# Attention over a node graph in fp32: the two heads of a pair computed side by side on TensorE

## The chip, the cores and the metric

The kernel runs on one core of a Trainium2 chip. The metric is the device time of one launch in microseconds (us), as the median of the runs. A profile of one execution on the same core comes with it. In it, PE is TensorE's matmul stream, PEld its loading of the stationary operand, DVE is VectorE, ACT is ScalarE, POOL is GpSimd and SP is SyncE.

## The reference

There are two layers over x[16, 1024, 256] (batch, nodes, channels), all in fp32, with one weighted adjacency matrix adj[1024, 1024] for all batches.

```python
# layer 0, HEADS = 4, hd = 64
fea = transpose(x, (0, 2, 1));  c_adj = mean(fea, axis=1)
diff = c_adj[:, None, :] - c_adj[:, :, None]
A = abs(abs(sigmoid(diff) - 0.5) - 0.5) * 2.0          # made symmetric
g = relu(einsum('bcn,bnm->bcm', fea, adj * A) * para)
q = heads of transpose(g);  k, v = heads of x @ kv_w
attn = softmax(einsum('bhnd,bhmd->bhnm', q, k) * scale, axis=-1)
out = einsum('bhnm,bhmd->bhnd', attn, v)
x = layernorm(x + out)
# layer 1: h = relu(x w_loop + adj (x w_neigh) + b), twice (256 -> 128 -> 256)
x = layernorm(x + (x + h) * 0.5)
```

The change lies in the attention of layer 0: for each batch and head, a 1024 by 1024 table of scores over 64 channels, its softmax over the last axis, and the product with the 64-wide values.

## The kernel before, in words

All constants, both forms of adj among them, stay on chip, and the kernel goes through the 16 batches in a Python loop that is written out into one straight program. A batch's 1024 nodes lie as eight blocks of 128 partitions. The steps of a batch are `attention`, a LayerNorm, `project` of the next batch (keys, values, and queries from the graph product `g_ps`), `graph_conv`, a second LayerNorm, and the store.

A tile framework assigns buffers from named pools. A pool tag has a fixed number of buffers (`bufs`), and an instruction that writes a new tile waits until the last reader of the tile that had the buffer is done. The framework also chooses the order in which the instructions stand on each engine; an engine then executes its own list in that order. So the order of the source isn't the order on PE: scores of a later tile stand between transposes and value products of an earlier one.

In `attention` the four heads are two pairs. The channels of a pair fill the 128 partitions: head s=0 has rows 0 to 63, head s=1 rows 64 to 127. A group is one pair and one half `j` of the nodes (512 queries, four blocks `i`). In a group, one head after the other does this:

- Scores (line 216): for each block `i`, two matmuls of 512 columns write a tile of 128 by 1024 into PSUM (`big`, two buffers of two banks each). The contraction is over 64 rows, so a matmul uses the upper or the lower half of the array's rows.
- Softmax: VectorE takes the negated maximum (line 219), ScalarE the exponential with the row's sum (line 221), into a `probs` tile (six buffers). The tile in PSUM is then free.
- For each of eight blocks `mt` of the keys: four transposes (line 226) into one bank (`bank`, three buffers), a copy to `pT` (lines 72 and 74, VectorE and ScalarE in turn; three buffers), and a value product (line 229) of 512 columns that accumulates into `pav[rows]`. It has 64 output channels, so it uses the left or the right half of the array's columns. `pav` has one buffer (tag `av`).

After both heads, `pav` is copied to `oT` (line 232), transposed back (line 237), scaled by the reciprocal of the sums and added to x (line 242). `wg` in `project` (lines 190 to 192) has three buffers of the size of a `probs` tile.

Of the kernel before, what the change touches and what calls it, by code (L numbers as in the profile page):

```python
# [10 lines left out]
F32 = mybir.dt.float32  # L11
AF = mybir.ActivationFunctionType
ALU = mybir.AluOpType
AX = mybir.AxisListType
# [3 lines left out]
def kernel(  # L18
# [11 lines left out]
    b2: bass.AP,  # L30
    out: bass.AP,
):
    """Graph attention with a LayerNorm, then a two-step graph convolution with a LayerNorm.

    A batch's nodes n = t * 128 + p lie on partition p, block t. The channel-major
    forms (suffix T) hold channels on partitions and nodes along the free axis.
    Everything of a batch stays on chip from its load to its store.
    """
    nc = tc.nc

    B, N, C = x.shape
# [18 lines left out]
    def big_psum(name):  # L60
        return psum.tile([P, N], F32, tag="big", name=name, bufs=2)
# [4 lines left out]
    turn = [0]  # L66

    def evacuate(dst, src):
        """Copy from PSUM, on the scalar and the vector engine in turn."""
        turn[0] ^= 1  # L70
        if turn[0]:
            nc.vector.tensor_copy(dst, src)  # L72
        else:
            nc.scalar.copy(dst, src)  # L74
# [3 lines left out]
        nc.sync.dma_start(out=xb, in_=x[b].rearrange("(t p) c -> p t c", p=P))  # L78
        return xb

# [1 line left out]
    x_next = load_x(0)  # L82
    adj_sb = const.tile([P, NT, N], F32, name="adj_sb")
    adj_v = adj.rearrange("(t p) m -> p t m", p=P)
# [38 lines left out]
                evacuate(adjT_sb[:, mt, ts(j, FB)], pt)  # L123

    def to_channel_major(src, name):
        """[node, channel] blocks to [channel, node]."""
        dst = work.tile([P, NC, N], F32, tag="xT", name=name, bufs=2)
        for cc in range(NC):
            for j in range(NJ):
                pt = bank_psum(f"{name}_ps_{cc}_{j}")  # L130
                for i in range(TJ):
                    nc.tensor.transpose(pt[:, ts(i, P)], src[:, j * TJ + i, ts(cc, P)], ident)  # L132
                evacuate(dst[:, cc, ts(j, FB)], pt)
        return dst

    def layernorm(xb, name):
        """In place over the channels of every node."""
        mv = small.tile([P, NT, 2], F32, tag="mv", name=f"mv_{name}", bufs=2)
        for t in range(NT):
            st = small.tile([P, nc.vector.BN_STATS_DIM], F32, tag="st", name=f"st_{name}_{t}")  # L140
            nc.vector.bn_stats(st, xb[:, t, :])
            nc.vector.bn_aggr(mv[:, t, :], st)
        rstd = small.tile([P, NT], F32, tag="rstd", name=f"rstd_{name}", bufs=2)
        nc.vector.tensor_scalar_add(rstd, mv[:, :, 1], EPS)
        nc.gpsimd.tensor_tensor(rstd, rstd, neg_half, ALU.pow)
        for t in range(NT):
            nc.vector.tensor_scalar(xb[:, t, :], xb[:, t, :], mv[:, t, 0:1], rstd[:, t:t + 1],  # L147
                                    op0=ALU.subtract, op1=ALU.mult)

    def project(b, xb):  # L150
        """Queries from the channel-weighted graph, keys and values of a batch."""
        xT = to_channel_major(xb, f"xT_{b}")

        # The channel mean of each node: along the free axis on all partitions, and per partition.
        pc = big_psum(f"mean_ps_{b}")
        for j in range(NJ):
            for cc in range(NC):
                nc.tensor.matmul(pc[:, ts(j, FB)], mean_w, xT[:, cc, ts(j, FB)],
                                 start=(cc == 0), stop=(cc == NC - 1))
        c_row = work.tile([P, N], F32, tag="c_row", name=f"c_row_{b}")  # L160
        nc.scalar.copy(c_row, pc)
        c_sum = small.tile([P, NT], F32, tag="c_sum", name=f"c_sum_{b}", bufs=2)
        nc.vector.tensor_reduce(c_sum, xb, AX.X, ALU.add)
        neg_c = small.tile([P, NT], F32, tag="neg_c", name=f"neg_c_{b}", bufs=2)
        nc.vector.tensor_scalar_mul(neg_c, c_sum, -1.0 / C)

        kT = work.tile([P, NC, N], F32, tag="kT", name=f"kT_{b}")
        for kb in range(NC):
            pk = big_psum(f"k_ps_{b}_{kb}")
            for j in range(NJ):  # L170
                for cc in range(NC):
                    nc.tensor.matmul(pk[:, ts(j, FB)], kvw_sb[:, cc, ts(kb, P)], xT[:, cc, ts(j, FB)],  # L172
                                     start=(cc == 0), stop=(cc == NC - 1))
            nc.scalar.copy(kT[:, kb, :], pk)

        v = work.tile([P, NT, C], F32, tag="v", name=f"v_{b}")
        per = N // C
        for g in range(NT // per):
            pv = big_psum(f"v_ps_{b}_{g}")
            for i in range(per):  # L180
                for cc in range(NC):
                    nc.tensor.matmul(pv[:, ts(i, C)], xT[:, cc, ts(g * per + i, P)], kvw_sb[:, cc, C:2 * C],  # L182
                                     start=(cc == 0), stop=(cc == NC - 1))
            nc.scalar.copy(v[:, g * per:(g + 1) * per, :], pv.rearrange("p (i c) -> p i c", c=C))

        # A[n, m] = 2 (0.5 - |sigmoid(d) - 0.5|) = 1 - tanh(|d| / 2), d = c[m] - c[n]; it is symmetric.
        pg = [big_psum(f"g_ps_{b}_{cb}") for cb in range(NC)]
        for t in range(NT):
            wg = work.tile([P, N], F32, tag="wg", name=f"wg_{b}_{t}", bufs=3)
            nc.scalar.activation(wg, c_row, AF.Abs, bias=neg_c[:, t:t + 1])  # L190
            nc.scalar.activation(wg, wg, AF.Tanh, scale=-0.5)  # L191
            nc.vector.scalar_tensor_tensor(wg, wg, 1.0, adj_sb[:, t, :], op0=ALU.add, op1=ALU.mult)  # L192
            for cb in range(NC):
                for j in range(NJ):
                    nc.tensor.matmul(pg[cb][:, ts(j, FB)], xb[:, t, ts(cb, P)], wg[:, ts(j, FB)],  # L195
                                     start=(t == 0), stop=(t == NT - 1))
        qT = work.tile([P, NC, N], F32, tag="qT", name=f"qT_{b}")
        for cb in range(NC):
            nc.vector.tensor_mul(qT[:, cb, :], pg[cb], para_sb[:, cb, :])
            nc.scalar.activation(qT[:, cb, :], qT[:, cb, :], AF.Relu, scale=QSCALE)  # L200
        return qT, kT, v

    def attention(b, xb, qT, kT, v):
        """Adds the heads' outputs to xb."""
        for pair in range(NC):
            for j in range(NJ):
                pav = psum.tile([P, FB], F32, tag="av", name=f"av_{b}_{pair}_{j}", bufs=1)
                den = small.tile([P, TJ, 2], F32, tag="den", name=f"den_{b}_{pair}_{j}", bufs=2)
                for s in range(2):
                    rows = slice(s * HD, (s + 1) * HD)  # L210
                    probs = []
                    for i in range(TJ):
                        t = j * TJ + i
                        ps = big_psum(f"s_{b}_{pair}_{t}_{s}")
                        for mj in range(NJ):
                            nc.tensor.matmul(ps[:, ts(mj, FB)], qT[rows, pair, ts(t, P)],  # L216
                                             kT[rows, pair, ts(mj, FB)], start=True, stop=True)
                        nmax = small.tile([P, 1], F32, tag="nmax", name=f"nmax_{b}_{pair}_{t}_{s}")
                        nc.vector.tensor_reduce(nmax, ps, AX.X, ALU.max, negate=True)  # L219
                        pr = work.tile([P, N], F32, tag="probs", name=f"pr_{b}_{pair}_{t}_{s}", bufs=6)  # L220
                        nc.scalar.activation(pr, ps, AF.Exp, bias=nmax, accum_out=den[:, i, s:s + 1])  # L221
                        probs.append(pr)
                    for mt in range(NT):
                        pt = bank_psum(f"pT_ps_{b}_{pair}_{j}_{s}_{mt}")
                        for i in range(TJ):
                            nc.tensor.transpose(pt[:, ts(i, P)], probs[i][:, ts(mt, P)], ident)  # L226
                        pT = work.tile([P, FB], F32, tag="pT", name=f"pT_{b}_{pair}_{j}_{s}_{mt}", bufs=3)
                        evacuate(pT, pt)
                        nc.tensor.matmul(pav[rows, :], v[:, mt, pair * P + s * HD:pair * P + (s + 1) * HD], pT,  # L229
                                         start=(mt == 0), stop=(mt == NT - 1))  # L230
                oT = work.tile([P, FB], F32, tag="oT", name=f"oT_{b}_{pair}_{j}", bufs=2)
                nc.scalar.copy(oT, pav)
# [11 lines left out]
                            xb[:, t, cols], op0=ALU.mult, op1=ALU.add)  # L244

    def graph_conv(b, xb):
        """Two graph convolutions on xb, and xb + (xb + h) / 2 into it."""
        xT = to_channel_major(xb, f"x1T_{b}")

        p1 = big_psum(f"t1_ps_{b}")  # L250
# [15 lines left out]
        h1T = work.tile([HID, N], F32, tag="h1T", name=f"h1T_{b}")  # L266
        nc.scalar.activation(h1T, ph, AF.Relu, bias=b1_sb)

        # adj (h1 w2) is taken as (adj h1) w2: h1 is half as wide.
        h1 = work.tile([P, NT, HID], F32, tag="hid", name=f"h1_{b}")  # L270
        for j in range(NJ):
            pt = bank_psum(f"h1n_ps_{b}_{j}")
# [67 lines left out]
```

## Time and profile before

| what | value |
|---|---|
| median of 2 runs | 4411.66 us (4403.0 and 4420.31) |
| span of the profiled execution | 4400.6 us |
| mean granted clock of TensorE | 0.987 |
| PE busy | 4244.0 us (96%) |
| PEld busy | 1872.7 us (43%) |
| DVE busy | 1618.8 us (37%) |
| ACT busy | 1448.9 us (33%) |

The profiled execution's span runs from its first to its last instruction. A launch's time has something around that span: the two runs lie 2.4 and 19.7 us above it. In the groups of the profile, a line names the source line, the engine, the operation, what is written and read with the shape, and the number of records; after the bar come the busy time and the mean length of one record, and then the idle time of that engine just ahead of the group, with what ended most of it. Matmuls are pipelined, so a record's length is more than the distance from its start to the next one's start.

### The profile page before, as it was taken

The page shows a single profiled execution, that of the slowest core. Times are in us where ns is not written, and L with a number is a line of the kernel's source. Part 1 is how long each engine was busy: PE and PEld are TensorE (multiplying, and loading weights), DVE is VectorE, ACT ScalarE, POOL GpSimd, SP SyncE. Part 2 cuts the span into 40 slices and gives each one's busy share as a digit, 9 for nine tenths or more (in the row PEclk, how much of TensorE's full clock was granted, in tenths as well). Part 3 has the DMA queues.
Part 4 walks back from the last instruction along what each step waited for, and adds up shares of the span by engine and source line. Part 5 has one row for each costly group of instructions (what it writes and reads, how often), then busy time and mean ns, then how long its engine had stood idle before and what let it go on. Part 6 is the DMA issues. An engine that isn't in the chain of part 4 may idle for free. (4 is left out here: it accounts for less than half of the span.)

```text
span 4400.6 us, 33372 instructions
## 1 busy us (share of the span) xinstructions
PE 4244.0 (96%) x13504; PEld 1872.7 (43%) x13504; DVE 1618.8 (37%) x2752; ACT 1448.9 (33%) x2161; POOL 53.4 (1%) x41
## 2 busy tenths in 40 slices
PE   8999999999999999999999999999999999999997
PEld 4344443444434344343443434434344343443433
DVE  3424434243342433424333243343433424344242
ACT  3333323334233342333423234233332333333231
POOL 0000000000000000000000000000000000000000
PEclk9999999999999999999999999999999999999999
DMA  2000000000000000000000000000000000000000
GB/s 77 1 1 19 1 20 0 0 20 1 20 1 0 20 1 19 1 1 19 1 19 1 1 20 1 20 1 10 10 1 19 1 12 8 1 19 1 10 0 10
DMA packets 36044, 41.98 MB, mean 10 GB/s; under 512 B 817, under 2 KB 34354, under 8 KB 35890
## 3 DMA queue, kind: packets, MB, share of 16 engines
q1 hardware_dynamic: 34802, 36.18, 2.5%
q10 hardware_dynamic: 1088, 3.67, 0.2%
q8 instruction: 106, 1.74, 0.2%
q14 instruction: 48, 0.39, 0.0%
HBM read 23.07 MB, written 16.78 MB: 9 GB/s over the span
## 5 line engine op out<-in xcount | busy, mean ns | idle before, releaser
L216 PE MATMUL s<-kT,qT 64*128 64x512 f32 x2048 | 1068.5, 630 | 8.7 <-ACT pr L221 8.7
L229 PE MATMUL av<-pT,v 128*64 128x512 f32 x2048 | 1034.8, 620 | 13.6 <-DVE pT L72 6.1
L219 DVE TENSOR_REDUCE nmax<-s 128x1 f32<-128x1024 f32 x512 | 625.9, 1222 | 667.8 <-PE s L216 665.8
L221 ACT ACTIVATE pr<-s,nmax 128x1024 f32<-128x1024 f32 x512 | 571.6, 1116 | 698.3 <-DVE nmax L219 698.2
L226 PEld LDWEIGHTS pT_ps<-ident,pr 128*128 128x128 f32 x4096 | 438.1, 141 | 684.0 <-issue 527.8
L226 PE MATMUL pT_ps<-ident,pr 128*128 128x128 f32 x4096 | 640.1, 285 | 44.1 <-ACT pr L221 36.9
L74 ACT COPY pT<-pT_ps 128x512 f32<-128x512 f32 x512 | 293.8, 587 | 1030.2 <-PE pT_ps L226 843.8
L72 DVE COPY pT<-pT_ps 128x512 f32<-128x512 f32 x512 | 346.9, 688 | 729.9 <-PE pT_ps L226 572.9
L216 PEld LDWEIGHTS s<-kT,qT 64*128 64x128 f32 x2048 | 332.8, 187 | 396.5 <-issue 348.6
L229 PEld LDWEIGHTS av<-pT,v 128*64 128x64 f32 x2048 | 233.8, 138 | 556.8 <-issue 233.6
L195 PE MATMUL g_ps<-wg,x 128*128 128x512 f32 x1024 | 442.1, 592 | 0.0
L195 PEld LDWEIGHTS g_ps<-wg,x 128*128 128x128 f32 x1024 | 194.6, 190 | 238.1 <-issue 233.4
L192 DVE SCALAR_TENSOR_TENSOR wg<-wg,adj_sb 128x1024 f32<-128x1024 f32 x128 | 156.0, 1225 | 358.0 <-ACT wg L191 358.0
L264 PE MATMUL h_ps<-adjT_sb,t 128*128 128x512 f32 x512 | 226.5, 595 | 3.6 <-ACT t L256 3.6
L279 PE MATMUL u_ps<-adjT_sb,h 128*128 128x512 f32 x512 | 224.0, 595 | 6.0 <-DVE h L72 3.7
L190 ACT ACTIVATE wg<-c_row,neg_c 128x1024 f32<-128x1024 f32 x128 | 145.1, 1145 | 115.8 <-PE g_ps L195 115.3
L242 DVE SCALAR_TENSOR_TENSOR x<-o_ps,rden,x 128x64 f32<-128x64 f32 x512 | 104.0, 276 | 150.1 <-PE o_ps L237 150.1
L264 PEld LDWEIGHTS h_ps<-adjT_sb,t 128*128 128x128 f32 x512 | 96.0, 190 | 131.3 <-issue 115.0
L279 PEld LDWEIGHTS u_ps<-adjT_sb,h 128*128 128x128 f32 x512 | 96.0, 190 | 124.6 <-issue 114.8
L72 DVE COPY h<-h1n_ps 128x512 f32<-128x512 f32 x16 | 11.1, 692 | 368.7 <-PE h1n_ps L274 368.7
L191 ACT ACTIVATE wg<-wg 128x1024 f32<-128x1024 f32 x128 | 134.2, 1054 | 2.5
L172 PE MATMUL k_ps<-xT,kvw_sb 128*128 128x512 f32 x256 | 113.8, 592 | 0.0
(68 smaller groups left out, 2043.5 us busy)
## 6 DMA issues: line engine op xcount, KB each, us to landing
x<-in_x_dram SPq DMA_DIRECT2D x16, 1024.0 KB, 5.7
out_dram<-x SPq DMA_DIRECT2D x16, 1024.0 KB, 4.4
adj_sb<-in_adj_dram SPq DMA_DIRECT2D x2, 1024.0 KB, 17.4
adj_sb<-in_adj_dram ACTq DMA_DIRECT2D x2, 1024.0 KB, 9.2
para_sb<-in_L_gnn_para_dram ACTq DMA_DIRECT2D x1, 1024.0 KB, 17.9
kvw_sb<-in_L_gnn_kv_w_dram ACTq DMA_DIRECT2D x1, 512.0 KB, 6.0
w1l_sb<-in_L_gnn_w_loop_dram SPq DMA_DIRECT2D x1, 128.0 KB, 19.1
w1n_sb<-in_L_gnn_w_neigh_dram SPq DMA_DIRECT2D x1, 128.0 KB, 15.1
```

The costliest lines, as they stand in the source:

```text
L72: nc.vector.tensor_copy(dst, src)
L74: nc.scalar.copy(dst, src)
L190: nc.scalar.activation(wg, c_row, AF.Abs, bias=neg_c[:, t:t + 1])
L192: nc.vector.scalar_tensor_tensor(wg, wg, 1.0, adj_sb[:, t, :], op0=ALU.add, op1=ALU.mult)
L195: nc.tensor.matmul(pg[cb][:, ts(j, FB)], xb[:, t, ts(cb, P)], wg[:, ts(j, FB)], start=(t == 0), stop=(t == NT - 1))
L216: nc.tensor.matmul(ps[:, ts(mj, FB)], qT[rows, pair, ts(t, P)], kT[rows, pair, ts(mj, FB)], start=True, stop=True)
L219: nc.vector.tensor_reduce(nmax, ps, AX.X, ALU.max, negate=True)
L221: nc.scalar.activation(pr, ps, AF.Exp, bias=nmax, accum_out=den[:, i, s:s + 1])
L226: nc.tensor.transpose(pt[:, ts(i, P)], probs[i][:, ts(mt, P)], ident)
L229: nc.tensor.matmul(pav[rows, :], v[:, mt, pair * P + s * HD:pair * P + (s + 1) * HD], pT, start=(mt == 0), stop=(mt == NT - 1))
L264: nc.tensor.matmul(ph[:, ts(j, FB)], t1[:, mt, :], adjT_sb[:, mt, ts(j, FB)], start=False, stop=(mt == NT - 1))
L279: nc.tensor.matmul(pu[:, ts(j, FB)], h1[:, mt, :], adjT_sb[:, mt, ts(j, FB)], start=(mt == 0), stop=(mt == NT - 1))
```

## The change

The two heads of a pair go through a group together. For each block `i`, the score matmuls alternate between head 0 and head 1 in the source (upper rows, lower rows), into two `big` tiles that are allocated together. All eight `probs` tiles of a group are made before the first value product in the source. For each `mt`, both heads' transposes and copies come first and then both value products, one into the left and one into the right columns' half of `pav`. `probs` and `wg` now share one tag `row` with ten buffers in place of six and three; `pT` has four buffers in place of three. The numbers and shapes of matmuls, transposes, copies, maxima and exponentials are the same as before.

```diff
-            wg = work.tile([P, N], F32, tag="wg", name=f"wg_{b}_{t}", bufs=3)
+            wg = work.tile([P, N], F32, tag="row", name=f"wg_{b}_{t}", bufs=10)
...
-                for s in range(2):
-                    rows = slice(s * HD, (s + 1) * HD)
-                    probs = []
-                    for i in range(TJ):
-                        t = j * TJ + i
-                        ps = big_psum(f"s_{b}_{pair}_{t}_{s}")
-                        for mj in range(NJ):
-                            nc.tensor.matmul(ps[:, ts(mj, FB)], qT[rows, pair, ts(t, P)],
+                heads = [slice(s * HD, (s + 1) * HD) for s in range(2)]
+                probs = {}
+                for i in range(TJ):
+                    t = j * TJ + i
+                    ps = [big_psum(f"s_{b}_{pair}_{t}_{s}") for s in range(2)]
+                    for mj in range(NJ):
+                        for s, rows in enumerate(heads):
+                            nc.tensor.matmul(ps[s][:, ts(mj, FB)], qT[rows, pair, ts(t, P)],
                                              kT[rows, pair, ts(mj, FB)], start=True, stop=True)
+                    for s in range(2):
                         nmax = small.tile([P, 1], F32, tag="nmax", name=f"nmax_{b}_{pair}_{t}_{s}")
-                        nc.vector.tensor_reduce(nmax, ps, AX.X, ALU.max, negate=True)
-                        pr = work.tile([P, N], F32, tag="probs", name=f"pr_{b}_{pair}_{t}_{s}", bufs=6)
-                        nc.scalar.activation(pr, ps, AF.Exp, bias=nmax, accum_out=den[:, i, s:s + 1])
-                        probs.append(pr)
-                    for mt in range(NT):
+                        nc.vector.tensor_reduce(nmax, ps[s], AX.X, ALU.max, negate=True)
+                        pr = work.tile([P, N], F32, tag="row", name=f"pr_{b}_{pair}_{t}_{s}", bufs=10)
+                        nc.scalar.activation(pr, ps[s], AF.Exp, bias=nmax, accum_out=den[:, i, s:s + 1])
+                        probs[s, i] = pr
+                for mt in range(NT):
+                    pTs = []
+                    for s in range(2):
                         pt = bank_psum(f"pT_ps_{b}_{pair}_{j}_{s}_{mt}")
                         for i in range(TJ):
-                            nc.tensor.transpose(pt[:, ts(i, P)], probs[i][:, ts(mt, P)], ident)
-                        pT = work.tile([P, FB], F32, tag="pT", name=f"pT_{b}_{pair}_{j}_{s}_{mt}", bufs=3)
+                            nc.tensor.transpose(pt[:, ts(i, P)], probs[s, i][:, ts(mt, P)], ident)
+                        pT = work.tile([P, FB], F32, tag="pT", name=f"pT_{b}_{pair}_{j}_{s}_{mt}", bufs=4)
                         evacuate(pT, pt)
-                        nc.tensor.matmul(pav[rows, :], v[:, mt, pair * P + s * HD:pair * P + (s + 1) * HD], pT,
+                        pTs.append(pT)
+                    for s, rows in enumerate(heads):
+                        nc.tensor.matmul(pav[rows, :], v[:, mt, pair * P + s * HD:pair * P + (s + 1) * HD], pTs[s],
                                          start=(mt == 0), stop=(mt == NT - 1))
```

## The prediction, made before the result was known

> **What bounds the kernel now.** I read the page first, its engine shares and then its costliest groups:
>
> ```profile
> PE 4244.0 (96%) x13504; PEld 1872.7 (43%) x13504; DVE 1618.8 (37%) x2752; ACT 1448.9 (33%) x2161; POOL 53.4 (1%) x41
> ...
> L216 PE MATMUL s<-kT,qT 64*128 64x512 f32 x2048 | 1068.5, 630 | 8.7 <-ACT pr L221 8.7
> L229 PE MATMUL av<-pT,v 128*64 128x512 f32 x2048 | 1034.8, 620 | 13.6 <-DVE pT L72 6.1
> L219 DVE TENSOR_REDUCE nmax<-s 128x1 f32<-128x1024 f32 x512 | 625.9, 1222 | 667.8 <-PE s L216 665.8
> L221 ACT ACTIVATE pr<-s,nmax 128x1024 f32<-128x1024 f32 x512 | 571.6, 1116 | 698.3 <-DVE nmax L219 698.2
> ...
> L226 PE MATMUL pT_ps<-ident,pr 128*128 128x128 f32 x4096 | 640.1, 285 | 44.1 <-ACT pr L221 36.9
> ```
>
> TensorE is the bound; VectorE and ScalarE wait for it. Scores (S, L216) use half the rows of the array (64*128), value products (V, L229) half its columns (128*64). Each has 1024 matmuls in the source and 2048 records here: an fp32 matmul is two records. Together they hold 2103 of 4244 busy us, and PE waited only 66.4 us (8.7+13.6+44.1) ahead of S, V and the transposes of the probabilities (T).
>
> Next, the timeline of PE inside a batch (start, length, records):
>
> ```profile
> 410.67 1.53 PE L226 MATMUL pT_ps<-ident,pr 128*128 128x128 f32 x12
> 412.16 2.79 PE L229 MATMUL av<-pT,v 128*64 128x512 f32 x6
> 414.88 1.09 PE L226 MATMUL pT_ps<-ident,pr 128*128 128x128 f32 x8
> 415.90 1.12 PE L216 MATMUL s<-kT,qT 64*128 64x512 f32 x2
> 416.96 1.93 PE L229 MATMUL av<-pT,v 128*64 128x512 f32 x4
> 418.82 3.70 PE L216 MATMUL s<-kT,qT 64*128 64x512 f32 x8
> 422.45 1.45 PE L226 MATMUL pT_ps<-ident,pr 128*128 128x128 f32 x9
> ```
>
> From start to next start, six V records take 2.72 us and four 1.86: 0.43 for each record, and 0.15 for each run whatever its length. S gives the same 0.43 and 0.2 a run (3.63 for eight, 1.06 for two); T gives 0.11 and 0.15 (1.49 for twelve, 1.02 for eight). A half-array record is thus as slow as a full one, and every change between S, V and T costs 0.15 to 0.2 us.
>
> Third, the timeline of what a score tile waits for, and the windows by stage:
>
> ```profile
> 420.83 1.22 DVE L219 TENSOR_REDUCE nmax<-s 128x1 f32<-128x1024 f32 x1 [2.55 <-PE s L216]
> ...
> 422.09 1.11 ACT L221 ACTIVATE pr<-s,nmax 128x1024 f32<-128x1024 f32 x1 [2.56 <-DVE nmax L219]
> ...
> 423.11 0.19 ACT L221 ACTIVATION_READ_ACCUMULATOR pr<-s,nmax 128x1 f32 x1
> ```
>
> ```profile
> 400.44:441.19 40.75, 40.65 (x133) 15.92 (x134) 16.88 (x25) 14.38 (x26) 0.00 (x0) 1.00 0.00 0
> ...
> 363.00:370.00 7.00, 7.00 (x10) 1.78 (x10) 0.56 (x1) 1.91 (x4) 0.00 (x0) 0.54 0.62 197
> ```
>
> A score tile is free for the next one 2.5 us after its last record (1.22, 0.03, 1.11, 0.1 for the accumulator's end, 0.05 to PE). The first window is one group (a pair, a half j of the nodes): 40.75 us, PE busy 40.65. The second shows the clock at 0.54 after a wait:
>
> ```profile
> 362.36 0.68 PE L226 MATMUL pT_ps<-ident,pr 128*128 128x128 f32 x3 [1.17 <-ACT pr L221]
> ```
>
> [...]
>
> **The change part by part.**
>
> *Alternation.* [...] I counted the neighbours in the orders of the two built programs. Before has none. After has 497 V alternations, but only 151 S ones, since the scheduler mostly gives each score tile both its 512-column halves at once, often with transposes before the other head.
>
> Of the 497, 377 have two or more transposes, or a score run, between the transposes of the second operand and the first product. Its copy (0.69 on VectorE, 0.59 on ScalarE) is then done about when B could start: I take 0.35 us, 377 x 0.35 = 132. The other 120 have that copy still running for 0.75 to 0.85 us after A starts, against 0.91 for A alone: 0.12 each, 14. Sum −146 us. I give S nothing: its alternations lie where the next score tile waits for its buffer (below); the other bound is 151 x 0.32 = 48.
>
> *Fewer runs.* S runs fall from 664 to 473, V runs from 616 to 527, transpose runs after them from 856 to 826: 191 x 0.2 + 89 x 0.15 + 30 x 0.15 = −56 us.
>
> *A longer score phase.* Before, four score tiles belong to a half-group, two computed ahead, and the other head's products fill the waits. Now eight stand together, and only three transposes of each i fit between (three banks). I laid one group out by hand from the durations above, t=0 at the last score run before the final products. First score 0 to 1.05; products to 2.91; oT's copy (3.05 to 3.64) precedes that tile's exponential on ScalarE, so its buffer frees at 4.9. Scores 2.91 to 3.96, o transposes to 4.55, scores of both heads to 7.31. On VectorE the eight L242 operations (1.63) stand ahead of the next maximum: 4.66 to 6.28, maximum to 7.5, exponential to 8.8. PE has three transposes to 7.79, then waits 1.02. Scores 8.81 to 12.43, transposes to 12.9, wait 0.47 for the buffer at 13.37; scores of i=3, then 0.25 for the last head-0 exponential; the last head-1 one is hidden by the next group's first scores. Sum 1.74 us, against 1.0 on average (66.4/64): +0.74 x 64 = +47. Bounds: 0 (all covered) to 3 us a group, +130.
>
> *Buffers.* probs and wg share ten tiles of 1024 where they had six and three: eight are live and two ahead, as before four and two. g_ps's matmuls had no idle time ahead (0.0); wg is done long before probabilities want its tiles. 0. pT with four instead of three: 0. No DMA is moved, and SP and POOL keep their order.
>
> *Clock.* The mean is 0.987: 1.3% of 4400 is 57 us, mostly one low stretch near each batch's start (1.17 us wait). There the new order has a score tile every 1.8 us and shorter waits, which may save 30; [...] I take 0, and keep −30 to +170.
>
> Sum: −146 −56 +47 = −155 on the profiled 4400.6, so 4246 as a span. The runs are 2.4 to 19.7 us above that span, their median 11.1: 4411.7 − 155 = 4257, −3.5%. 2% (88 us) is about what a measurement tells from no change.
>
> **The rivals.**
>
> *No overlap in fp32.* The 146 go: 4403, no change. For it: nothing in this trace shows two tiles at once. [...]
>
> *Every alternation restarts like a run: slower.* [...] 497 x 0.15 + 151 x 0.2 = 105 us come on top of 4403: 4508. Place: between the two products of each mt. From 0.15 us an alternation it decides (648 x 0.15 = 97, to 4500). For: the first record of each run in this trace exposes its load. [...]
>
> *The throttle.* The 1.02 us wait lies among scores[...]. If each of 64 groups loses 3.4 us less the 0.7 of waits it then covers, 173: 4430 with overlap, 4576 without. [...]
>
> **How the numbers follow.** Overlap 0.54 (4257; own range 4205 to 4325); no overlap 0.23 (4403); restart 0.13 (4508); throttle 0.10 (4430 or 4576, half each). Faster by 2% is below 4323: nearly all of the first, 0.51. Slower is above 4500: restart and half of the throttle, 0.19. Within: 0.30. The range 4200 to 4500 leaves out some 0.06 below and 0.14 above.
>
> **What would show it.** In the timeline, a V run of four should take 1.5 us to the next start where before's took 1.86, with the second head's first record starting about 0.1 us after the first head's second. The busy time of the V group should fall by some 150 us and that of S by little; idle time ahead of S should rise from 8.7 to about 100 us, released by the exponential. An unchanged 0.43 between all V records means no overlap; over 0.5 at the change of head means restarts. A mean clock below 0.97 means the throttle. I am wrong most easily on fp32 tiles not overlapping, or on VectorE's order making the score phase wait longer.

## The result, and the profile after

The changed kernel takes 4557.1 us (median of two runs, 4554.8 to 4559.3) against 4411.7 before: 1.034 times as long, with a 95% interval of 1.031 to 1.037. The profiled execution spans 4557.6 us. The forecast was 4257, with a range to 4500.

The page of the kernel after, its engine shares, the granted clock in 40 slices, and the three PE groups of attention (line 218 scores, 236 value products, 231 transposes):

```profile
PE 4302.4 (94%) x13504; PEld 1944.0 (43%) x13504; DVE 1612.1 (35%) x2752; ACT 1433.1 (31%) x2161; POOL 53.4 (1%) x41
...
PEclk8897987989879898798988989789897898978888
...
L218 PE MATMUL s<-kT,qT 64*128 64x512 f32 x2048 | 1211.1, 792 | 135.1 <-ACT pr L224 134.6
L236 PE MATMUL av<-pT,v 128*64 128x512 f32 x2048 | 865.5, 668 | 28.7 <-DVE pT L72 9.3
...
L231 PE MATMUL pT_ps<-ident,pr 128*128 128x128 f32 x4096 | 690.7, 306 | 1.7 <-DVE x L249 0.4
```

The value products did fall, from 1034.8 busy us to 865.5. The scores rose from 1068.5 to 1211.1, and the wait ahead of them from 8.7 to 135.1. The new thing is the clock: its mean is 0.888 where it was 0.987. In the clock records of both traces every stretch is at half clock or at full, so that is 2 x 0.112 x 4558 = 1021 us at half clock, against 2 x 0.013 x 4401 = 114 before.

The timeline of PE in one group shows both sides, first the overlap, then the loss:

```profile
399.31 1.56 PE L236 MATMUL av<-pT,v 128*64 128x512 f32 x4
400.81 0.87 PE L231 MATMUL pT_ps<-ident,pr 128*128 128x128 f32 x6
...
402.66 1.08 PE L236 MATMUL av<-pT,v 128*64 128x512 f32 x4
403.67 1.12 PE L218 MATMUL s<-kT,qT 64*128 64x512 f32 x2
...
407.47 0.55 PE L231 MATMUL pT_ps<-ident,pr 128*128 128x128 f32 x3
409.47 4.87 PE L218 MATMUL s<-kT,qT 64*128 64x512 f32 x8 [1.45 <-ACT pr L224]
414.27 0.90 PE L231 MATMUL pT_ps<-ident,pr 128*128 128x128 f32 x3
415.10 3.78 PE L218 MATMUL s<-kT,qT 64*128 64x512 f32 x4
```

Four product records took 1.86 us to the next start before. Here they take 1.50 where the second head's copy comes late (399.31), and 1.01 where both operands are ready (402.66): two slots for four records, a full overlap. Ready pairs are the minority: of the 394 such runs at full clock in the trace, 72 took 1.01 us, 72 took 1.37, 146 took 1.49 and 87 took 1.80, with a mean of 1.45. Then, after a wait of 1.45 us among the scores, a run of four score records takes 3.7 us instead of 1.9. The windows of that stretch and of the rest of the group give the clock (the number after the five engines):

```profile
403.82:411.00 7.18, 5.73 (x19) 2.84 (x21) 4.06 (x11) 4.03 (x7) 0.00 (x0) 0.98 0.00 0
411.00:434.00 23.00, 23.00 (x39) 7.41 (x36) 6.49 (x7) 5.79 (x10) 0.00 (x0) 0.50 0.00 1
434.00:451.20 17.20, 16.82 (x76) 7.68 (x76) 5.18 (x7) 3.52 (x6) 0.00 (x0) 0.98 0.00 0
```

The clock is halved from just after the wait to the end of the scores and comes back only in the value products. PE is busy throughout, so its busy share of 94% hides it. The trace's clock record has 57 such stretches, 17.9 us long on average. Of these, 38 begin 4 to 14 us after a group's copy of `oT`, that is, in the score phase that follows; most of the others lie in the scores of a batch's first group.

### The profile page after: what moved, and what is told of

The parts are those of the page before. It is cut to its first block, busy times and chain, and to the rows that moved or that the text cites. A ratio compares the mean times of both kernels' runs of the same rounds, so it can differ in the third digit from the quotient of the medians.

```text
span 4557.6 us, 33427 instructions
## 1 busy us (share of the span) xinstructions
PE 4302.4 (94%) x13504; PEld 1944.0 (43%) x13504; DVE 1612.1 (35%) x2752; ACT 1433.1 (31%) x2161; POOL 53.4 (1%) x41
## 4 chain that ended last, share of the span: by engine, by line
PE 82%; DVE 8%; ACT 7%; issue 1%; POOL 0%; DMA 0%; ACTq 0%; POOLq 0%; DVEq 0%
PE s L218 19%; PE av L236 18%; PE pT_ps L231 10%; PE g_ps L195 10%; PE u_ps L286 5%; PE h_ps L271 5%; DVE nmax L222 4%; ACT pr L224 3%; PE v_ps L182 2%; PE k_ps L172 2%; ACT pT L74 2%; PE h_ps L298 2%; PE h_ps L296 2%; DVE x L249 2%; PE t_ps L260 1%; PE h_ps L297 1%
## 5 line engine op out<-in xcount | busy, mean ns | idle before, releaser
L218 PE MATMUL s<-kT,qT 64*128 64x512 f32 x2048 | 1211.1, 792 | 135.1 <-ACT pr L224 134.6
L236 PE MATMUL av<-pT,v 128*64 128x512 f32 x2048 | 865.5, 668 | 28.7 <-DVE pT L72 9.3
L231 PEld LDWEIGHTS pT_ps<-ident,pr 128*128 128x128 f32 x4096 | 485.9, 153 | 759.6 <-issue 741.1
L231 PE MATMUL pT_ps<-ident,pr 128*128 128x128 f32 x4096 | 690.7, 306 | 1.7 <-DVE x L249 0.4
L218 PEld LDWEIGHTS s<-kT,qT 64*128 64x128 f32 x2048 | 400.2, 230 | 569.4 <-issue 352.5
L195 PE MATMUL g_ps<-wg,x 128*128 128x512 f32 x1024 | 442.1, 592 | 0.0
L236 PEld LDWEIGHTS av<-pT,v 128*64 128x64 f32 x2048 | 188.9, 143 | 394.0 <-ACT pT L74 167.5
L199 DVE TENSOR_TENSOR qT<-g_ps,para_sb 128x1024 f32<-128x1024 f32 x32 | 39.2, 1225 | 279.4 <-PE g_ps L195 279.4
L200 ACT ACTIVATE qT<-qT 128x1024 f32<-128x1024 f32 x32 | 33.9, 1059 | 316.2 <-DVE qT L199 316.2
```

Of the source, the lines that this page charges most:

```text
L218: nc.tensor.matmul(ps[s][:, ts(mj, FB)], qT[rows, pair, ts(t, P)], kT[rows, pair, ts(mj, FB)], start=True, stop=True)
L231: nc.tensor.transpose(pt[:, ts(i, P)], probs[s, i][:, ts(mt, P)], ident)
```

## The experiments

The theory from the two traces: the clock goes down on the waits among the scores, because the scores use only half the array's rows, and then stays low for the rest of the score phase. Rival 1: two tiles at work at once draw the clock down. Rival 2: any wait of about 1 us does it, whatever stands around it. Rival 3: the waits themselves cost the time, not the clock.

**Stages of matmuls alone.** A kernel with nothing but 512-column fp32 matmuls on the same data; `warm` is 32 matmuls on the full array.

```diff
+    def run(stage, mms):       # one PSUM tile, copied out by ScalarE at the end; the next run waits for that
+    for _ in range(24):
+        run("gaprow", [(lo, full, k % 2) for k in range(4)])       # rows, columns, bank
+    warm()
...                              # likewise gapfull; gapcol: (full, (lo, hi)[k // 2], k % 2); gaprows: (lo, hi)[k % 2], eight of them
+    run("onerow", [(lo, full, k % 2) for k in range(96)])
+    run("tworows", [((lo, hi)[k % 2], full, k % 2) for k in range(192)])
...                              # likewise onecol, twocols
```

> This kernel leaves the layers out: it runs matmuls of 512 columns in stages with full-array matmuls between them, and copies x to the output. Four stages wait for a ScalarE copy of about 1.0 us after every short run (four matmuls on half the rows; four on the full array; four on half the columns; eight that alternate the row halves), four run 96 or 192 matmuls without a wait (one row half; alternating row halves; one column half; alternating column halves). Theory (waits among half-array matmuls bring the throttle): the stages without a wait keep clock 1.00, the alternating ones take 0.43 us for each two records; the waiting half-row stages fall to a mean clock below 0.7, and the waiting full-array stage stays clearly higher. Rival 1 (two tiles at once draw the clock down): the alternating stages without a wait are low, the waiting stage on one row half is as the full-array one. Rival 2 (any wait of 1 us brings it): all four waiting stages are alike.

The windows of the eight stages, in this order: waiting on one row half, on the full array, on the two column halves, on alternating row halves; then without waits one row half, alternating row halves, one column half, alternating column halves:

```profile
45.00:229.00 184.00, 158.54 (x178) 55.14 (x177) 22.26 (x22) 0.00 (x0) 0.50 0.33 108
262.50:377.60 115.10, 88.19 (x191) 34.48 (x192) 23.28 (x23) 0.00 (x0) 1.00 0.00 0
408.30:481.30 73.00, 45.93 (x190) 12.07 (x192) 23.28 (x23) 0.00 (x0) 1.00 0.00 0
512.10:627.50 115.40, 88.26 (x384) 35.06 (x384) 23.28 (x23) 0.00 (x0) 1.00 0.00 0
658.10:740.20 82.10, 82.06 (x191) 35.82 (x192) 0.00 (x0) 0.00 (x0) 1.00 0.00 0
770.90:852.90 82.00, 82.00 (x382) 37.05 (x384) 0.00 (x0) 0.00 (x0) 1.00 0.00 1
883.60:965.60 82.00, 82.00 (x192) 26.20 (x192) 0.00 (x0) 0.00 (x0) 1.00 0.00 0
996.20:1078.20 82.00, 81.97 (x382) 27.49 (x384) 0.00 (x0) 0.00 (x0) 1.00 0.00 1
```

The only low clock, 0.50, is that of the runs on one row half with waits. PE's waits are about 1.2 us there (25.5 us in 22 waits). The full array with the same runs, the same copies and waits as long stays at 1.00, so rival 2 falls for waits of this length. The stage on column halves is not the same work: its runs use both halves, which overlap, so PE is busy for 46 us instead of 88. One column half alone with waits was not run. The alternating stages stay at 1.00 too, with waits and without. Without waits they do twice as many records as one half does in the same 82 us: 0.21 us a record instead of 0.43, in rows and in columns alike. Rival 1 falls. DMA was busy beside the first stage (0.33), but the next kernel shows the low clock without it.

**The low clock and what ends it.** The same frame, with other runs.

```diff
+        run("short", [(lo, full, 0) for k in range(4)])             # 24 times, copy of 512 columns
+        run("long", [(lo, full, k % 2) for k in range(8)])          # 16 times
+        run("again", [(lo, full, k % 2) for k in range(4)])         # 10 times, then:
+    run("halfback", [(lo, full, k % 2) for k in range(64)])
+    run("colback", [(full, (lo, hi)[k // 2 % 2], k % 2) for k in range(32)])
```

> As the first stages kernel (layers left out, matmuls in stages, x copied to the output). Runs of four matmuls on one row half with a shorter wait (a copy of 512 columns, about 0.6 us); runs of eight with the wait of the first stages kernel; then ten runs of four with that wait, to bring the low clock, followed by 64 matmuls on one row half without a wait and 32 on column halves. Theory: [...] the longer runs stay at 1.00 or fall less often than the runs of four did; the shorter wait lies between. Once low, the half-row stretch without a wait keeps it low [...] (as the scores of the changed kernel did), and the column halves bring it back. Rival 4 [...]: the half-row stretch runs at 0.43 us a record [...].

The windows of the long runs, of the row-half stretch without a wait, and of the column halves after it:

```profile
259.80:481.00 221.20, 204.69 (x235) 75.52 (x234) 14.17 (x14) 0.00 (x0) 0.50 0.00 0
...
590.00:698.00 108.00, 108.00 (x127) 42.24 (x128) 0.00 (x0) 0.00 (x0) 0.50 0.00 0
704.00:715.00 11.00, 11.00 (x54) 4.60 (x52) 0.00 (x0) 0.00 (x0) 1.00 0.00 0
```

Two expectations were misses. Long runs fall to 0.50 as well, and so do short waits (0.7 us): 0.50 over 167 us of their stage, after 1.00 in its first 11 us. So no wait that one row half bears was found. And the row-half stretch, which was expected to stay low for a time only, doesn't recover: all 64 matmuls, 108 us without any wait, ran at half clock, though the same stream had stayed at 1.00 when it began at 1.00. Rival 4 falls with it: 0.85 us a record. Work on one row half without waits kept the clock that it found, 1.00 for 82 us in the first kernel and 0.50 for 108 us in this one.

**Full rows in the changed kernel.** The scores contract over 128 rows, with zeros in the other head's rows of the queries. The scores' numbers stay, and so does the order on PE but for 36 of 13504 records.

```diff
+    qz = [const.tile([P, NC, N], F32, name=f"qz_{s}") for s in range(2)]
+    for s in range(2):
+        nc.vector.memset(qz[s][(1 - s) * HD:(2 - s) * HD, :, :], 0.0)
...
+                nc.scalar.activation(qz[s][own, cb, :], qm[own, :], AF.Relu, scale=QSCALE)
...
-                            nc.tensor.matmul(ps[s][:, ts(mj, FB)], qT[rows, pair, ts(t, P)],
-                                             kT[rows, pair, ts(mj, FB)], start=True, stop=True)
+                            nc.tensor.matmul(ps[s][:, ts(mj, FB)], qT[s][:, pair, ts(t, P)],
+                                             kT[:, pair, ts(mj, FB)], start=True, stop=True)
...
-        dst = work.tile([P, NC, N], F32, tag="xT", name=name, bufs=2)
+        dst = work.tile([P, NC, N], F32, tag="xT", name=name, bufs=1)
```

> The changed kernel with scores on all 128 rows: the other head's 64 rows of the stationary queries are zero, so each score matmul gives the same numbers, takes the same 0.43 us a record, stands in the same place and waits for the same buffers; two heads can't overlap any more. Theory (half-row matmuls with waits between them keep the clock low): mean clock above 0.96; the time falls although the scores lose their overlap, to 4150 to 4350 us. Rival 2 (the waits bring the throttle whatever the rows): clock 0.87 to 0.90, 4550 to 4700 us.

Measured: 4161.7 us (four runs), clock 0.995, 0.944 of before (interval 0.941 to 0.946). The groups of scores (now line 224) and products (242) on its page:

```profile
L224 PE MATMUL s<-kT,qz 128*128 128x512 f32 x2048 | 982.1, 606 | 129.4 <-ACT pr L230 129.4
...
L242 PE MATMUL av<-pT,v 128*64 128x512 f32 x2048 | 791.6, 617 | 29.3 <-ACT pT L74 8.8
```

PE waits for the exponential about as long as in the changed kernel, 129.4 us to 135.1 in sum and 2.0 to 2.4 at the longest, and yet the low clock is nearly gone. This is the decisive run: with waits alike and other rows, 395 us come off, although the scores no longer overlap (eight records took 3.62 us to the next start, 0.45 each). Rivals 2 and 3 fall in the kernel itself. The rows change two more things, which pull in opposite directions. The scores lose their overlap; and now that they have the array shape of the transposes (128*128), a change between the two was measured at next to nothing: a score run between two transpose runs took 0.195 us beyond its records in before, and 0.003 here. The clock record tells the balance. Of the 1211.1 busy us of scores in the changed kernel, 612 lay at half clock, so 306 were lost to it; at full clock they would have been an estimated 905, fewer than the 982.1 here. The 395 thus doesn't overstate what the low clock cost.

**No row maximum, changed kernel and kernel before.** Both take the exponential of the plain score with bias 0, so part of the softmax's work is left out.

```diff
-                        nc.vector.tensor_reduce(nmax, ps[s], AX.X, ALU.max, negate=True)
...
-                        nc.scalar.activation(pr, ps[s], AF.Exp, bias=nmax, accum_out=den[:, i, s:s + 1])
+                        nc.scalar.activation(pr, ps[s], AF.Exp, bias=zero_col, accum_out=den[:, i, s:s + 1])
```

> The changed kernel with the row maximum left out (exponential of the plain score, bias 0), so a score tile is free 1.3 us after its last record instead of 2.5. Theory: PE hardly waits ahead of the scores (under 20 us instead of 135), the mean clock returns to above 0.97, and the time falls to 3950 to 4100 us. Rival 1 (two tiles at once draw the clock down): clock stays near 0.89, time 4350 to 4450. Rival 3 (the time went into PE's waits themselves, not the clock): 135 us less, about 4420.

> The kernel before with the row maximum left out (exponential of the plain score, bias 0): the control of after_nomax. Theory: little to win here, as PE waited 66 us in all around the scores: 4280 to 4400 us, clock 0.98 to 1.00; so most of what after_nomax gained over the changed kernel is the clock and the overlap. Rival 3 (leaving the maximum out is itself worth hundreds of us): below 4150 us.

Measured, one run each: 3948.7 us at clock 0.997 for the changed kernel, and 4244.4 at 0.997 for the kernel before. PE's waits ahead of the changed kernel's scores fell to 56.3 us, not below 20. The control is a miss too: leaving the maximum out was worth 168 us there, not up to 130. The comparison is also not clean, since with shorter waits the scheduler orders the scores anew (427 changes of head within score runs instead of 151). What stands: with the maximum out of both, the change gains 296 us where it lost 145, and the shorter waits no longer come with a low clock.

**Transposes added where PE waits.**

```diff
-                            nc.tensor.transpose(pt[:, ts(i, P)], probs[s, i][:, ts(mt, P)], ident)
+                            for _ in range(4 if mt == 0 else 1):
+                                nc.tensor.transpose(pt[:, ts(i, P)], probs[s, i][:, ts(mt, P)], ident)
```

> The changed kernel with the transposes of block mt=0 issued four times each (same result), so that more transposes stand among the scores where PE waits: 1536 more matmul records, 167 us of PE work at 0.109 each. Theory: the added work lies in the waits and keeps the clock up: mean clock above 0.94, time falls in spite of it, to 4250 to 4450 us. Rivals 1 and 3: the clock is as before or the work is simply added, 4560 to 4720 us.

Measured: 4446.7 us (one run), clock 0.951. With 1536 more matmul records, the kernel is 110 us faster than the changed one, at the edge of what was expected. PE's line of its page:

```profile
PE 4192.6 (94%) x15040; PEld 2056.2 (46%) x15040; DVE 1609.5 (36%) x2752; ACT 1438.3 (32%) x2161; POOL 53.4 (1%) x41
```

More records take less busy time (4192.6 to 4302.4), which goes with the higher clock. But the waits weren't filled: 132.4 us of waiting for the exponential ahead of the scores are left of 134.6. The low stretches are nearly as many, 50 instead of 57, and half as long, 8.7 us on average instead of 17.9. So the added transposes did not prevent the low clock, they ended it sooner.

**The scores' part alone**, with the value products of the two heads one after the other again.

```diff
-                for mt in range(NT):
-                    pTs = []
-                    for s in range(2):
+                for s, rows in enumerate(heads):
+                    for mt in range(NT):
...
-                        pTs.append(pT)
-                    for s, rows in enumerate(heads):
-                        nc.tensor.matmul(pav[rows, :], v[...], pTs[s],
+                        nc.tensor.matmul(pav[rows, :], v[...], pT,
```

> One part alone: all scores of a group side by side as in the changed kernel, but the value products one head after the other as in the kernel before. Theory: the low clock comes from the score phase, so the mean clock stays at 0.87 to 0.91, and the products lose their overlap: 4650 to 4800 us. Rival 1 with the product pairs as its cause: clock above 0.95 and 4350 to 4500 us.

Measured: 4733.9 us (one run), clock 0.896. So the low clock comes without the product pairs too, 0.896 against 0.888 with them; taking them apart costs 177 us even at the low clock.

**A version that feeds the scores in between.** The next group's scores go, two heads of one block at a time, between the value products of the present group; 16 `row` tiles hold two groups' probabilities and, to make room, five other tiles (`c_row`, `t1`, `h1T`, `h1`, `uT`), with fewer buffers for `xT`, `pT` and `r`.

```diff
+            for mt in range(NT):
...
+                if nxt and mt % 2 == 0:
+                    score_pair(*groups[n + 1], mt // 2, *nxt)
+                for s, rows in enumerate(heads):
+                    nc.tensor.matmul(pav[rows, :], v[...], pTs[s],
```

> The changed kernel with the next group's scores, two heads of one block together, between the value products of the present one (two key blocks apart), so that no score waits for its buffer beside idle rows; 16 tiles for probabilities and other rows of 4 KB. Theory: mean clock above 0.97, waits ahead of scores under 40 us, overlap in the products and in more scores: 3750 to 4000 us. Rivals 1 and 2: the clock stays below 0.93 and the time above 4200 us.

Measured: 3956.8 us, 0.898 of before (0.895 to 0.900), clock 0.940. The time is as expected, but the clock is lower, and the waits ahead of the scores longer (67.1 us), than was expected. The timeline of PE in a group (line 212 scores, 244 products, 237 transposes):

```profile
364.52 1.99 PE L212 MATMUL s<-kT,qT 64*128 64x512 f32 x8
366.43 1.08 PE L244 MATMUL av<-pT,v 128*64 128x512 f32 x4
367.44 1.53 PE L237 MATMUL pT_ps<-ident,pr 128*128 128x128 f32 x12
```

Eight score records now take 1.91 us to the next start, where before took 3.63. What stays low is mainly the first group of each batch, whose scores still stand alone (from 335.98, four score records take 3.7 us).

**That first group on full rows**, the queries padded with zeros as above.

```diff
+        qz = work.tile([P, 2, FB], F32, tag="row", name=f"qz_{b}", bufs=16)
+        nc.gpsimd.memset(qz, 0.0)
+        for s, rows in enumerate(heads):
+            nc.scalar.copy(qz[rows, s, :], qT[rows, 0, 0:FB])
...
+                    if whole:
+                        nc.tensor.matmul(ps[s][:, ts(mj, FB)], qz[:, s, ts(i, P)], kT[:, pair, ts(mj, FB)],
```

> The pipelined version with the first group of each batch, whose scores still stand alone, on all 128 rows (zeros for the other head, as in the full-rows kernel). Theory: the low stretch at the start of each batch (some 25 us each in the pipelined version) goes, the mean clock rises from 0.94 to above 0.985, and the time falls by 120 to 220 us to 3740 to 3840 us. Rival 2 (waits bring the throttle whatever the rows): clock and time as the pipelined version, about 3957 us.

Measured: 3933.9 us, 0.894 of before (0.893 to 0.896), clock 0.975. Both expectations were missed. The clock rose, but the time hardly fell: the two versions' intervals overlap. The group of those scores and the start of one batch on the timeline of PE tell why:

```profile
L219 PE MATMUL s<-kT,qz 128*128 128x512 f32 x512 | 275.7, 686 | 119.7 <-ACT pr L228 119.6
...
554.32 3.70 PE L219 MATMUL s<-kT,qz 128*128 128x512 f32 x8
563.87 6.54 PE L219 MATMUL s<-kT,qz 128*128 128x512 f32 x8 [5.85 <-ACT pr L228]
```

In these 16 stretches PE waits 119.7 us for the softmax, more than the version without the padding waited ahead of all its scores (67.1). And full rows are no protection from a wait as long as the 5.85 us here: at 13 of the 16 batches it stands in this place, and the clock is at half for most of the next eight records, which take 6.54 us instead of the 3.70 of those ahead of the wait. So rival 2 falls for the scores' waits of up to 2.0 us that the full-rows kernel bore, and not for any wait.

## Why the prediction was wrong

*What bounds the kernel* held: PE did, before and after. But the busy time of a PE group contains its clock (four score records took 3.7 us at half clock and 1.9 at full), and the prediction took the clock for a small item.

*The failed step* is "Clock. ... I take 0", with the rival "The throttle" at a chance of 0.10 and a price of 173 us. The mechanism was named there, with its place, the wait among the scores. Its chance and its size were wrong. The price supposed the low stretch that before has at 362.6: 6.8 us at half clock, so 3.4 lost. There, value products followed soon after the wait:

```profile
364.98 5.00 PE L229 MATMUL av<-pT,v 128*64 128x512 f32 x6
```

Value products ran in the last 6.8 us of 12 of the 18 low stretches in the clock record of before, and of 48 of the 57 in that of the changed kernel (the one above ends at 434.6, in a run of six). In the stages too the clock was at 1.00 again on column halves (704.0 to 715.0). In the new score phase row-half scores and a few transposes follow first, and a stretch lasts 17.9 us on average, where the one at 362.6 lasted 6.8. Full rows at waits alike give the size: 4557.1 − 4161.7 = 395 us. The clock record gives it a second way: half of 1021 us less half of 114 is some 450 us of PE's time, part of which would have been waits at full clock. With 395 in place of 0, the forecast of 4257 becomes 4652; the remaining 95 is about what the steps below were short by (−252 against −155). That the 4557 measured lies close to the 4576 forecast under "The throttle" without overlap is luck: the overlap came, and the low clock cost more than twice its price (395 against 173).

The same step hoped for shorter waits near a batch's start, worth 30 us. The opposite came, since all scores of a batch's first group now stand together:

```profile
357.83 5.01 PE L218 MATMUL s<-kT,qT 64*128 64x512 f32 x8 [2.44 <-ACT pr L224]
```

The wait there is 2.44 us instead of 1.17, and the low stretch after it 27.3 us long.

*Alternation* was right in kind, and its sum too small. The forecast took 0.35 us of the 1.86 for a ready pair: the author's estimate for one of the four records running beside another, which the trace of before doesn't show. In the run at 402.66 the four start at 402.663, 402.670, 403.143 and 403.150, so the second head's first record runs beside the first head's first, and a ready pair gains 0.85. The 1.5 us that the forecast named is the commonest length, but by luck: at 399.31 it comes from the second head's copy, which ends at 399.75, just before that head starts at 399.80. With the clock up, the products' busy time fell by 243 us (1034.8 to 791.6). Some 24 of these were low clock in before and 13 are saved run starts, which leaves about 206 for the overlap, or 0.41 for each of 497 alternations, against the 146 of the forecast.

The scores, which it gave nothing with 48 as the other bound, gained too: from 1068.5 us before, less 15 of low clock and 38 of saved run starts, to the 905 estimated above is some 110 for their overlap. The rivals of no overlap and of restarts fell: 0.21 us a record in the alternating stages.

*A longer score phase* was right in kind: waits in a group, released by the exponential. Ahead of S, V and T, PE waited 165.5 us after (135.1 + 28.7 + 1.7) against 66.4, so +99 against the +47 taken, and inside the bound of 130. With full rows, at full clock, it was 186.5 (129.4 + 29.3 + 27.8), so +120.

*Fewer runs* and *Buffers*: no run tells them apart from the rest. No new wait on `wg` or `pT` showed: g_ps has 442.1 busy us and no idle time in both pages.

*The sum without the clock*: full rows gives 4160.6 − 4400.6 = −240 as a span. The rise of the clock from 0.987 to 0.995 explains some 35 of it (half of 114 less half of 42), which leaves about −205 against the forecast −155. This lacks the overlap of the scores and has instead the cheap changes between scores and transposes. By its parts, the changed kernel at full clock comes to an estimated −206 (overlap of the products) −110 (overlap of the scores) −56 (fewer runs, as forecast) +120 (waits) = −252.

Open: why work on one row half with waits loses the clock (0.50) where the full array keeps it (1.00). The runs show that it does, not why. They don't show which waits full rows bear either: the scores of the full-rows kernel bore 2.0 us, those of the last version didn't bear 5.85, and in before a wait of 1.18 us on full rows, soon after two of 0.68, was followed at four of the 16 batches by a low clock, 0.67 over the eight records of `mean_ps` from 249.68 to 254.91 at the first of them.

## What to carry to other kernels

Before work is regrouped on half the array's rows, ask what stands in its waits: here row-half matmuls with waits of 0.7 to 1.2 us among them ran at a clock of 0.50, and a stretch of them alone, 108 us long, didn't regain it. Three things helped here: alternating the two row halves (1.00 in the stages), other work between them (0.940 with value products, 0.951 with transposes, against 0.888), and padding the contraction with zeros (0.995). The padded version was 9% faster than the one that used fewer rows. And read the granted clock next to PE's busy share: PE was 94% busy here at a clock of 0.888.

## What the runs showed that was not expected

- Two fp32 matmuls on different row halves, or on different column halves, ran fully side by side: 0.21 us a record against 0.43.
- Runs on one row half with waits of about 1.2 us, or of 0.7 with a shorter copy, halved the clock (0.50); with waits of 1.2 us, the same runs on the full array, and runs that alternate the row halves, didn't (1.00).
- A stream on one row half, without any wait, stayed at full clock for 82 us where it started there, and stayed at half clock for all of its 108 us when it started low.
- Rows padded with zeros kept the clock up as well: 0.995 against 0.888, with half of the stationary operand zero.
- On full rows a wait of 5.85 us was followed by half clock all the same: eight records took 6.54 us instead of 3.70.
- The price of a change between scores and transposes went with the change of shape: 0.195 us for a score run of 64*128 between transposes of 128*128, 0.003 for one of 128*128.
